# Widths of the node ranges of edge tiles: fixed for blocks of 32 edge tiles instead of 128

## The chip, the cores and the metric

The kernel runs on one core of a Trainium2 chip. A core has a matmul engine (TensorE: PE in the profile, with its weight loads as PEld), a vector engine (VectorE: DVE), a scalar engine (ScalarE: ACT), a general engine (GpSimd: POOL) and a queue engine that issues transfers (SyncE: SP). Data lies in HBM (DRAM), in SBUF (128 partitions) and in PSUM, where matmuls write[...]. The metric is the device time of one execution in microseconds (us); of several runs the median counts.

## The reference, cut to what matters

A graph with 6250 nodes of 256 features and 100,000 edges goes through three relational layers (8 edge types) and one attention layer, each with a residual sum and a layer norm. All values are fp32. The edges are sorted by `dst`, and `dst` is 6250 times the square of a uniform number: low nodes have many edges, high nodes few.

```python
dst = jnp.minimum((6250 * jax.random.uniform(...) ** 2.0).astype(jnp.int32), 99999)
_o = jnp.argsort(dst, stable=True)
src = src[_o]; dst = dst[_o]
...
for l in range(n_layers):                       # 3 layers
    xr = jnp.einsum('nd,rde->rne', x, W_rel[l])
    msg = xr[edge_type, src]
    agg = jax.ops.segment_sum(msg, dst, num_segments=x.shape[0])
    x = jax.nn.relu(agg + x @ W_root[l] + bias[l])
```

After the layers: `x = layernorm(x0 + x)`, then attention with 4 heads over the first 6250 edges, `x = layernorm(x + attention)`.

## The kernel before

**Tiles and windows.** The 100,000 edges are cut into T = 782 edge tiles of 128 edges. Because edges are sorted by `dst`, the 128 edges of one tile end in a short range of nodes. The kernel gives each tile a window: W neighbouring node numbers, from the tile's least `dst` on. For a tile the kernel gathers the 128 source rows (128 x 256, one indirect DMA from POOL), builds a one-hot matrix of 128 edges x (8 types x W nodes), and multiplies: rows transposed times one-hot. That sums the rows by type and node. The product, 2 halves of 128 features x 8 W columns, is then added into a ring `S` in SBUF at the place of the tile's first node. When all edge tiles of a node tile (128 nodes) have been added, a dense step multiplies the sums with the weights of the 8 types and with the root weight.

**Widths.** W must be known when the program is built. `Plan.W` holds one width per chunk of 128 edge tiles (CH = 7 chunks). It takes the density of nodes at the chunk's last edge, times 128 edges, plus five standard deviations and 2 (lines 56 to 60). For this graph the list is 6, 10, 14, 18, 21, 25, 26. `WMAX` is 26. Four places read it: the one-hot (line 474), the window matmuls (499), the add (517), and the tables: `wm` (W - 1 for each tile, lines 303 to 305), which bounds the window's start (`most`, line 312) and enters the test for tiles whose edges don't fit (line 400), and the key of an edge, type x W + node within the window (line 356). If any tile doesn't fit, a flag sends the program into a second, general path after the fast one. The first 36 tiles (TH) are not done in windows but through a count matrix `A` (`count`, `products`), so windows are made for 746 tiles.

**Order.** `Plan.order` puts the tiles into groups of four (GT), 188 groups, high tiles first, and alternates two streams: f = 0 has tiles 410 to 781, f = 1 has tiles 36 to 409; each stream has its own ring (4 and 3 node tiles long). The order is the same in each of the three layers and the layers are issued one after another in the written order (`manual_schedule`). Before the layers, `tables` computes indices, keys and positions; its instructions are ordered by the framework.

In step i of a layer (loop at line 774) the kernel issues:
- four gathers on POOL (`gather`, line 492) into one of eight `msg` buffers, and the positions of the four windows (`places`);
- on DVE the one-hot of the group four steps later (`onehot`, line 476);
- what follows finished dense steps (`finish`: bias, relu, store; in the last layer a layer norm too), and clearing the ring's rows on ACT;
- on PE the window matmuls of group i (`windows`, line 509), into banks `pw`, of which there are four. As many windows share a bank as fit, rounded down to 4, 2 or 1 (lines 501 and 502): 4 for W up to 8, 2 for W up to 16, else 1;
- a piece of the waiting dense steps (`dense`, lines 573 and 577, into `pd`);
- on DVE the four adds into the ring (`add`, line 521);
- transposes and the start of new dense steps for node tiles that have become complete.

The last layer has more on PE and DVE (`logits`, and from step 164 on `prepare`, which takes `msg` buffers and `pw` banks too). `products` loads node rows into `msg` buffers from step 130 on. The gathers of a layer read the table that the layer before has stored. After the layers comes `attention`.

Of the kernel before, what the change touches and what calls it, by code (L numbers as in the profile page):

```python
# [10 lines left out]
F32 = mybir.dt.float32  # L11
# [3 lines left out]
ALU = mybir.AluOpType  # L15
# [5 lines left out]
P = 128  # L21
# [11 lines left out]
DB = 32  # L33
PREP_AT = 164
PIECE = 6
AHEAD = 4
LEAD = 6
GWIN = 256
# [4 lines left out]
class Plan:  # L43
# [7 lines left out]
    def __init__(self, N, E, R):  # L51
        self.N, self.E = N, E
        self.NT = (N + P - 1) // P
        self.T = (E + P - 1) // P
        self.CH = (self.T + P - 1) // P
        self.W = []
        for c in range(self.CH):
            f = min(1.0, (c + 1) * P * P / E)
            step = 2.0 * N * f / E
            self.W.append(min(PAD, math.ceil(P * step + 5 * math.sqrt(P) * step + 2)))  # L60
        self.WMAX = max(self.W)

        self.TH = 0
        while self.hot_high(self.TH) < HOT - 0.01:
            self.TH += 1
        self.TH -= self.TH % GT


        mid = (self.T + self.TH) // 2
        self.TM = min(range(mid - 16, mid + 16),  # L70
                      key=lambda t: (len(self.shared(t)), abs(t - mid)))
# [86 lines left out]
def fast(tc, const, pl, x, xs, src, dst, edge_type, w_rel, w_root, bias, weight,  # L158
# [10 lines left out]
    with ExitStack() as top:  # L169
# [26 lines left out]
        with tc.tile_pool(name="ps_p", bufs=2, space=PSUM) as ps_p:  # L196
            tables(tc, pl, ps_p, src, dst, edge_type, ident, idx, key, pos, iota, iota_p,
                   lane, hk, hl, hif, dt, flag, R, H)
        y = dram.tile([NT * P, D], F32, name="y")

        with ExitStack() as s:
            wp = s.enter_context(tc.tile_pool(name="wp", bufs=1))
            sp = s.enter_context(tc.tile_pool(name="sp", bufs=1))
            mp = s.enter_context(tc.tile_pool(name="mp", bufs=8))
            op = s.enter_context(tc.tile_pool(name="op", bufs=AHEAD + 2))
            xp = s.enter_context(tc.tile_pool(name="xp", bufs=3))
# [44 lines left out]
def tables(tc, pl, ps_t, src, dst, edge_type, ident, idx, key, pos, iota, iota_p, lane, hk, hl,  # L251
           hif, dt, flag, R, H):

    nc = tc.nc
    E, NT, T, CH, WMAX = pl.E, pl.NT, pl.T, pl.CH, pl.WMAX
    TF = E // P
    with tc.tile_pool(name="prep", bufs=1) as prep:
# [29 lines left out]
        sf, df, tf = flt  # L287
# [5 lines left out]
        def turned(o, f, c0, c1):  # L293
            pt = ps_t.tile([P, 4 * P], F32, name="pt")
            for c in range(c0, c1):
                nc.tensor.transpose(pt[:, (c - c0) * P:(c - c0 + 1) * P], f[:, c], ident)
            nc.vector.tensor_copy(o[:, c0 * P:c1 * P], pt[:, :(c1 - c0) * P])
# [3 lines left out]
            turned(idx, sf, c0, c1)  # L301

        wm = prep.tile([P, CH], F32, name="wm")
        for c in range(CH):
            nc.vector.memset(wm[:, c:c + 1], float(pl.W[c] - 1))

        lim = float(pl.N) / float(E) ** 2
        most = prep.tile([P, CH], F32, name="most")
# [23 lines left out]
        def place(o, c0, c1):  # L332

            m0, m1 = pl.TM // P, (pl.TM + P - 1) // P
            if min(c1, m1) > c0:
                remainder(o[:, c0:min(c1, m1)], c0, min(c1, m1), NS[1])
            if c1 > max(c0, m1):
                remainder(o[:, max(c0, m1):c1], max(c0, m1), c1, NS[0])
            if m0 < m1 and c0 <= m0 < c1:
                up = prep.tile([P, 1], F32, name="up")  # L340
                m = prep.tile([P, 1], F32, name="m")
                remainder(up, m0, m1, NS[0])
                nc.vector.tensor_scalar(m, tn[:, m0:m1], float(pl.TM) - 0.5, None, op0=ALU.is_gt)
                nc.vector.tensor_tensor(up, up, o[:, m0:m1], ALU.subtract)
                nc.vector.scalar_tensor_tensor(o[:, m0:m1], up, m, o[:, m0:m1],
                                               op0=ALU.mult, op1=ALU.add)

        for c0, c1 in parts:
            nc.vector.tensor_copy(df[:, c0:c1], raw[1][:, c0:c1])
            nc.scalar.copy(tf[:, c0:c1], raw[2][:, c0:c1])  # L350
            nc.vector.tensor_reduce(lo[:, c0:c1], df[:, c0:c1], AX.X, ALU.min)
            nc.vector.tensor_tensor(
                sf[:, c0:c1], df[:, c0:c1],
                lo[:, c0:c1].unsqueeze(2).to_broadcast([P, c1 - c0, P]), ALU.subtract)
            for c in range(c0, c1):
                nc.vector.scalar_tensor_tensor(sf[:, c], tf[:, c], float(pl.W[c]), sf[:, c],
                                               op0=ALU.mult, op1=ALU.add)
            turned(key, sf, c0, c1)

            nc.vector.tensor_tensor(at[:, c0:c1], lo[:, c0:c1], least[:, c0:c1], ALU.max)  # L360
            nc.vector.tensor_tensor(at[:, c0:c1], at[:, c0:c1], most[:, c0:c1], ALU.min)
            place(posf, c0, c1)
            pr = ps_t.tile([P, 4 * P], F32, name="pt")
            for c in range(c0, c1):
                nc.tensor.matmul(pr[0:1, (c - c0) * P:(c - c0 + 1) * P], posf[:, c:c + 1], ident,
                                 start=True, stop=True)
            nc.vector.tensor_copy(pos[0:1, c0 * P:c1 * P], pr[0:1, :(c1 - c0) * P])
# [28 lines left out]
        b = prep.tile([P, CH], F32, name="b")  # L396
# [59 lines left out]
def layer(tc, pl, l, final, groups, ready, S, hold, A, hk, hl, idx, key, pos, iota, ident, wr, wo,  # L456
          bias_b, x, xs, eps, w1x, altab, y, att, mp, op, xp, hp, ps_w, ps_d, ps_t, H):
    nc = tc.nc
    N, D = x.shape
    KC = D // P  # L460
    R = wr.shape[2]
# [9 lines left out]

    def onehot(i):
        g = groups[i][1]
        w = R * pl.W[g[0] // P]
        oh = op.tile([P, GT, R * pl.WMAX], F32, name="oh")
        nc.vector.tensor_tensor(  # L476
            oh[:, :len(g), :w], iota[:, :w].unsqueeze(1).to_broadcast([P, len(g), w]),
            key[:, g[0]:g[-1] + 1].unsqueeze(2).to_broadcast([P, len(g), w]), ALU.is_equal)
        return oh

    def places(i):
        f, g = groups[i]
        _, v = nc.values_load_multi_w_load_instructions(
            pos[0:1, g[0]:g[-1] + 1], engines=[DVE], min_val=0, max_val=NS[f] * P - 1,
            skip_runtime_bounds_check_because="a remainder of the ring's size")
        return v
# [9 lines left out]

    def windows(i, msg, oh):
        g = groups[i][1]
        w = R * pl.W[g[0] // P]

        nb = 512 // (KC * w)
        nb = 4 if nb >= 4 else 2 if nb >= 2 else 1
        res = []
        for n, (q, t) in enumerate(reversed(list(enumerate(g)))):
            if n % nb == 0:
                pb = ps_w.tile([P, 512], F32, name="pw")
            pw = pb[:, (n % nb) * KC * w:(n % nb + 1) * KC * w]
            for k in range(KC):
                nc.tensor.matmul(pw[:, k * w:(k + 1) * w], msg[:, q, k * P:(k + 1) * P],  # L509
                                 oh[:, q, :w], start=True, stop=True)  # L510
            res.append((q, t, pw))
        return res

    def add(i, wins, vals):
        f, g = groups[i]
        n = NS[f]
        W = pl.W[g[0] // P]
        for q, t, pw in wins:
            a, b = pl.touched(t)
            o = S[f][:, :, ds(vals[q], W)]  # L520
            ins = nc.vector.tensor_tensor(  # L521
                o, o, pw.rearrange("p (a b) -> p a b", b=W), ALU.add)
            for j in done[f][-n:]:
                assert j > b
                if all((j - m) % n for m in range(a, b + 1)):
                    tc.declare_no_dep(ins.ins, group=f"used{l}_{f}_{j}",
                                      reason="the window lies in other node tiles of the ring")
            for h, j in ready:
                assert (h != f or j <= b or j in done[f]
                        or j % n not in [m % n for m in range(a, b + 1)])  # L530
# [233 lines left out]
    for j, (i, f) in last.items():  # L764
        early.setdefault(max(0, i - 2), []).append(j)
    held, turned, xTs = {}, [], {}
    ohs = [onehot(i) for i in range(min(AHEAD, NG))]
    fin, log = [], []
    counting = count() if l == 0 else iter(())
    hot = products()  # L770
    prep = prepare() if final else iter(())
    if final:
        nc.vector.memset(altab, 0.0)
    for i in range(NG + 5):
# [10 lines left out]
        if i < NG:  # L785
            msg = gather(i)
            vals = places(i)
        if i + AHEAD < NG:
            ohs.append(onehot(i + AHEAD))
        for j, yt in [t for k, t in log if k <= i - 2]:  # L790
# [8 lines left out]
        if i < NG:  # L799
            wins = windows(i, msg, ohs.pop(0))  # L800

        n = PIECE * max(1, len(turned)) if i < NG else KC * (R + 1)
        while turned and n > 0:
# [4 lines left out]
        if i < NG:  # L808
            add(i, wins, vals)
# [519 lines left out]
```

## Time and profile before

| what | value |
|---|---|
| median of 3 runs | 3013.36 us (3005.31 to 3019.54) |
| the profiled execution | 3008.72 us, its span 3007.0 us |
| mean granted TensorE clock | 0.941 |
| ACT busy | 462.7 us (15%) |
| mean DMA rate | 129 GB/s |

The stages can be read from the first and last gather of each layer and from the share of time in which the engines are busy. Layer 0 gathers from 11.0 to 947.4 us, layer 1 from 968.3 to 1902.8, layer 2 from 1923.5 to 2883.5; attention and the end take the rest to 3007. The page's forty slices show the same: PE stays at nine tenths or more for most slices, with dips at the two layer boundaries and in the end.

```profile
PE   5999999999987799999988988789999999998874
POOL 6777777777775777777777777577767777777723
PEclk9999999999988999999999987899999999999875
```

Each digit is the busy share of a slice of 75 us in tenths. "Idle before" in the groups and the view of waits name what ended an engine's idle time; "issue" there means that the engine waited for nothing that the profile shows. The chain of waits is followed back from the last instruction; its shares name the engine that each stretch of it was spent on.

### The profile page before, as it was taken

Reading aid. Unit: us, or ns where it says so; the run is one execution under the profiler, and the core shown is the slowest. Engines: PE = TensorE matmul, PEld = TensorE weight load, DVE = VectorE, ACT = ScalarE, POOL = GpSimd, SP = SyncE. Lnnn points to the kernel's source line nnn. Section 1 sums busy time; section 2 is a strip of 40 time slices with the busy share of each in tenths; the row PEclk is TensorE's granted clock in tenths of the full one; section 3 lists DMA queues with packets and bytes.
Section 4 is the critical chain, followed back from the end, with each engine's and each line's share of the span. In section 5 each row is a group of like instructions: output and inputs, shape, how many; then the busy total and the mean of one; then the engine's idle time right before and its main releaser. Section 6 shows DMA issues by size and latency. Waiting matters only on the chain.

```text
span 3007.0 us, 45570 instructions
## 1 busy us (share of the span) xinstructions
PE 2692.7 (90%) x15710; PEld 2444.4 (81%) x15711; DVE 1735.3 (58%) x4084; ACT 462.7 (15%) x611; POOL 2158.3 (72%) x2258
## 2 busy tenths in 40 slices
PE   5999999999987799999988988789999999998874
PEld 4989888889876798999877887688888888888763
DVE  7646677775443555555455444356666656655775
ACT  2111111111001111111111110011111111111015
POOL 6777777777775777777777777577767777777723
PEclk9999999999988999999999987899999999999875
DMA  4444444445433444444444543344444444455523
GB/s 151 125 124 122 120 117 122 120 134 172 134 114 116 119 123 120 125 122 122 119 118 146 166 125 114 118 124 127 131 120 128 123 127 127 152 169 153 167 89 130
DMA packets 203055, 389.00 MB, mean 129 GB/s; under 512 B 42885, under 2 KB 128004, under 8 KB 202820
## 3 DMA queue, kind: packets, MB, share of 16 engines
q0 software_dynamic: 107424, 293.48, 33.6%
q1 hardware_dynamic: 87464, 85.04, 8.8%
q10 hardware_dynamic: 7932, 7.48, 0.7%
q8 instruction: 131, 2.15, 0.3%
q14 instruction: 104, 0.85, 0.1%
HBM read 360.18 MB, written 25.65 MB: 128 GB/s over the span
## 4 chain that ended last, share of the span: by engine, by line
PE 74%; POOL 6%; issue 6%; DVE 6%; DMA 5%; ACT 2%; DVEq 0%; ACTq 0%; POOLq 0%; SPq 0%
PE pw L509 34%; PE pd L577 31%; POOL msg L492 6%; PE pd L573 4%; DMA msg<-x,idx 3%; DVE S L521 3%; PE pd L681 1%; PE pt L544 1%; DMA msg<-in_x_dram,idx 1%; PE pt L625 1%; ACT xT L547 1%; ACT o L1028 1%; PE pd L652 1%; DVE oh L476 0%; PE p L1006 0%
## 5 line engine op out<-in xcount | busy, mean ns | idle before, releaser
L492 POOL DMA_INDIRECT msg<-x,idx x1492 | 1417.9, 950 | 518.2 <-issue 409.4
L521 DVE TENSOR_TENSOR S<-S,pw 128x224 f32 (+6 forms) x2238 | 953.8, 426 | 947.4 <-PE pd L577 519.4
L509 PE MATMUL pw<-oh,msg 128*128 128x112 f32 (+6 forms) x8952 | 1337.4, 305 | 176.8 <-DMA msg<-x,idx 89.1
L509 PEld LDWEIGHTS pw<-oh,msg 128*128 128x128 f32 x8952 | 1272.6, 200 | 247.6 <-DVE S L521 108.8
L577 PE MATMUL pd<-wr,S 128*128 128x256 f32 x4704 | 1103.7, 385 | 1.3 <-DVE S L521 1.3
L577 PEld LDWEIGHTS pd<-wr,S 128*128 128x128 f32 x4704 | 892.2, 193 | 117.3 <-DVE S L521 2.5
L492 POOL DMA_INDIRECT msg<-in_x_dram,idx x746 | 708.6, 950 | 237.8 <-issue 204.4
L476 DVE TENSOR_TENSOR oh<-iota,key 128x672 f32<-128x672 f32 (+8 forms) x564 | 388.2, 690 | 20.6 <-issue 9.8
L586 ACT ACTIVATE S<-S 128x2048 uint32<-128x2048 uint32 x150 | 285.0, 1900 | 0.1
L547 ACT COPY xT<-pt 128x256 f32<-128x256 f32 x195 | 72.3, 371 | 1001.3 <-PE pt L544 1001.3
L594 ACT ACTIVATE h<-pd 128x256 f32<-128x256 f32 x98 | 37.6, 384 | 915.2 <-DVE pd L591 735.1
L573 PE MATMUL pd<-wo,xT 128*128 128x256 f32 x588 | 164.9, 405 | 3.8 <-ACT h L594 3.8
L591 DVE TENSOR_TENSOR pd<-pd,bias_b 128x256 f32<-128x256 f32 x147 | 63.0, 428 | 168.9 <-PE pd L577 168.7
L573 PEld LDWEIGHTS pd<-wo,xT 128*128 128x128 f32 x588 | 108.5, 201 | 13.2 <-ACT h L594 4.3
L643 DVE TENSOR_SCALAR sel<-iota,hk 128x392 bf16<-128x392 f32 x138 | 80.3, 613 | 0.0
L608 ACT ACTIVATE rs<-mv,eps 128x1 f32<-128x1 f32 x49 | 14.4, 295 | 418.9 <-DVE mv L607 418.9
L681 PE MATMUL pd<-msg,A 128*128 128x256 f32 x294 | 70.3, 381 | 1.7 <-DMA msg<-x 1.7
L1010 POOL TENSOR_TENSOR z<-yg,td 128x1536 f32<-128x1536 f32 (+1 forms) x9 | 29.4, 3274 | 56.7 <-DVE bn L988 28.0
L681 PEld LDWEIGHTS pd<-msg,A 128*128 128x128 f32 x294 | 54.6, 192 | 8.5 <-issue 2.0
L544 PE MATMUL pt<-ident,xin 128*128 128x128 f32 x294 | 58.2, 281 | 1.9 <-ACT xT L547 1.4
L625 PEld LDWEIGHTS pt<-w1x,xT 128*128 128x128 f32 x192 | 25.4, 193 | 35.1 <-ACT xT L547 35.1
L544 PEld LDWEIGHTS pt<-ident,xin 128*128 128x128 f32 x294 | 41.7, 146 | 13.6 <-ACT xT L547 2.6
(186 smaller groups left out, 671.7 us busy)
## 6 DMA issues: line engine op xcount, KB each, us to landing
msg<-x,idx POOLq DMA_INDIRECT x1492
x<-h SPq DMA_DIRECT2D x96, 128.0 KB
xin<-x SPq DMA_DIRECT2D x96, 128.0 KB
msg<-x SPq DMA_DIRECT2D x24, 512.0 KB
msg<-in_x_dram,idx POOLq DMA_INDIRECT x746
y<-yt SPq DMA_DIRECT2D x49, 128.0 KB
wr<-in_L_gnn_W_rel_dram ACTq DMA_DIRECT2D x6, 1024.0 KB
xin<-in_x_dram SPq DMA_DIRECT2D x48, 128.0 KB
```

The lines of the kernel that those rows point to most:

```text
L476: nc.vector.tensor_tensor(oh[:, :len(g), :w], iota[:, :w].unsqueeze(1).to_broadcast([P, len(g), w]), key[:, g[0]:g[-1] + 1].unsqueeze(2).t ...
L492: nc.gpsimd.indirect_dma_start(out=msg[:, q, :], out_offset=None, in_=table, in_offset=bass.IndirectOffsetOnAxis(ap=idx[:, t:t + 1], axis=0))
L509: nc.tensor.matmul(pw[:, k * w:(k + 1) * w], msg[:, q, k * P:(k + 1) * P], oh[:, q, :w], start=True, stop=True)
L521: ins = nc.vector.tensor_tensor(o, o, pw.rearrange("p (a b) -> p a b", b=W), ALU.add)
L544: nc.tensor.transpose(pt[:, k * P:(k + 1) * P], t[:, k * P:(k + 1) * P], ident)
L547: nc.scalar.copy(xT.rearrange("p k n -> p (k n)"), pt[:, :D])
L573: nc.tensor.matmul(pd[:, :D], xT[:, k], wo[:, k], start=(k == 0), stop=False)
L577: i = nc.tensor.matmul(pd[:, :D], s[:, k * R + r], wr[:, k, r], start=False, stop=(k == KC - 1 and r == R - 1))
L586: i = nc.scalar.memzero(cols(f, j))
L591: nc.vector.tensor_tensor(pd[:, :D], pd[:, :D], bias_b[:, l], ALU.add)
L643: nc.vector.tensor_scalar(oh, iota[:, :NT * R], float(512 * n), hk[:, t:t + 1], op0=ALU.add, op1=ALU.is_equal)
L681: nc.tensor.matmul(ph[:, :D], A[:, j], t[:, n], start=(n == 0), stop=(j == js[-1]))
```

## The change

The widths are fixed for blocks of 32 edge tiles (WB = 32) instead of chunks of 128. `Plan.W` now has 28 entries, by the same formula, with the density at the block's last edge: 3, 4, 5, ... rising by about one a block to 26. All readers index it with the tile divided by 32. Since one column of the tables holds 128 tiles on the partitions, `wm` is filled with one memset of 32 partitions for each block, 28 in place of 7, and a new column table `wn` (W itself) takes the place of the number in the key's formula. WMAX, the order of the groups, the streams and the positions of everything else stay. Groups of four tiles never cross a block.

The widths of the tiles that are done in windows, block by block, and how many windows share a bank:

| tiles | W before | W after (blocks of 32) | windows in a bank, before -> after |
|---|---|---|---|
| 36-127 | 6 | 4, 5, 6 | 4 -> 4 |
| 128-255 | 10 | 7, 8, 9, 10 | 2 -> 4, 4, 2, 2 |
| 256-383 | 14 | 11, 12, 13, 14 | 2 -> 2 |
| 384-511 | 18 | 15, 16, 17, 18 | 1 -> 2, 2, 1, 1 |
| 512-639 | 21 | 19, 20, 20, 21 | 1 -> 1 |
| 640-767 | 25 | 22, 23, 24, 25 | 1 -> 1 |
| 768-781 | 26 | 26 | 1 -> 1 |

```diff
+WB = 32
...
-        for c in range(self.CH):
-            f = min(1.0, (c + 1) * P * P / E)
+        for c in range(self.CH * P // WB):
+            f = min(1.0, (c + 1) * WB * P / E)
             step = 2.0 * N * f / E
             self.W.append(min(PAD, math.ceil(P * step + 5 * math.sqrt(P) * step + 2)))
...
         wm = prep.tile([P, CH], F32, name="wm")
-        for c in range(CH):
-            nc.vector.memset(wm[:, c:c + 1], float(pl.W[c] - 1))
+        for b, w in enumerate(pl.W):
+            p0 = b * WB % P
+            nc.vector.memset(wm[p0:p0 + WB, b * WB // P:b * WB // P + 1], float(w - 1))
+        wn = prep.tile([P, CH], F32, name="wn")
+        nc.vector.tensor_scalar(wn, wm, 1.0, None, op0=ALU.add)
...
-                nc.vector.scalar_tensor_tensor(sf[:, c], tf[:, c], float(pl.W[c]), sf[:, c],
+                nc.vector.scalar_tensor_tensor(sf[:, c], tf[:, c], wn[:, c:c + 1], sf[:, c],
                                                op0=ALU.mult, op1=ALU.add)
...
     def onehot(i):
         g = groups[i][1]
-        w = R * pl.W[g[0] // P]
+        w = R * pl.W[g[0] // WB]
...
     def windows(i, msg, oh):
         g = groups[i][1]
-        w = R * pl.W[g[0] // P]
+        w = R * pl.W[g[0] // WB]
...
     def add(i, wins, vals):
-        W = pl.W[g[0] // P]
+        W = pl.W[g[0] // WB]
```

## The prediction

> **What bounds the kernel now.** I read the page first, then the waits of POOL layer by layer, then short stretches of the timeline where POOL stood still, and last the groups by shape, for prices.
>
> ```profile
> PE 2692.7 (90%) x15710; PEld 2444.4 (81%) x15711; DVE 1735.3 (58%) x4084; ACT 462.7 (15%) x611; POOL 2158.3 (72%) x2258
> PE 74%; POOL 6%; issue 6%; DVE 6%; DMA 5%; ACT 2%; DVEq 0%; ACTq 0%; POOLq 0%; SPq 0%
> L492 POOL DMA_INDIRECT msg<-x,idx x1492 | 1417.9, 950 | 518.2 <-issue 409.4
> ```
>
> Busy shares and the chain of waits both say TensorE. But the last line has the gathers of layers 1 and 2 (L492), and behind its 0.95 us each stands idle time that is put down to "issue": POOL waited for nothing. The timeline shows a fixed rhythm, 0.95 us busy and 0.30 us of issue, so a gather costs 1.25 us. There are 746 edge tiles in each of three layers, 2238 gathers: 2238 x 1.25 = 2798 us of the 3007 us span, 93%. The waits of POOL, first in layer 1 (969 to 1903 us), then in layer 2 (1924 to 2884 us), with columns total us, times, longest:
>
> ```profile
> POOL msg L492 <- issue: 208.6, 684, 0.6
> POOL msg L492 <- DMA wr<-in_L_gnn_W_rel_dram: 20.0, 1, 20.0
> POOL msg L492 <- PE pw L509: 10.1, 33, 0.3
> ...
> POOL msg L492 <- issue: 200.7, 659, 0.3
> POOL msg L492 <- PE pw L509: 30.1, 43, 4.2
> POOL msg L492 <- DMA wr<-in_L_gnn_W_rel_dram: 19.7, 1, 19.7
> POOL msg L492 <- DMA msg<-x,idx: 7.8, 14, 3.9
> POOL msg L492 <- PE pt L544: 6.0, 11, 2.4
> ```
>
> In layer 1 no wait but the layer boundary is longer than 0.6 us: waits on PE of at most 0.3 us are the issue gap itself under another name. So POOL never stood still for PE there: 745 intervals took 934.5 us (968.32 to 1902.85), 1.254 each. Layer 0 took 936.4 (11.03 to 947.40). Layer 2 took 960.0 (1923.54 to 2883.53), 25 more, and there POOL does wait for PE, up to 4.2 us:
>
> ```profile
> 2238.39 0.94 POOL L492 DMA_INDIRECT msg<-x,idx  x1 [3.96 <-PE pw L509]
> ```
>
> The gathers write eight `msg` buffers; a ninth group has to wait until the windows matmuls have read the oldest. So PE sets the pace only where it is eight groups behind. From the starts of all gathers I add up what each interval has above 1.25 us: layer 0, 1.8 us (387 to 470 us); layer 1, nothing; layer 2, 10.0 us between 2219 and 2369, 3.3 at 2592 and 2653, and 10.9 from 2806 on, after `prepare` has begun to take `msg` buffers too. That is 26 us in all, the most that a faster PE or DVE can take out of the gather stream. The rest (11.0 us head, two boundaries of 20.9 and 20.7, 123.5 from the last gather to the end) is no matter of window widths, but for some tenths.
>
> **What the Trainium skill says.** Perfetto Trace Analysis, Identifying the Most-Contended Engine, takes occupancy as the measure for GPSIMD and warns against matmul busy time. The warning fits; the occupancy (72%) does not: with the issue gaps POOL is at 93%. TensorE: Matmul & The Clock Gate, Back-to-back issue gap, says that in a stream of load and matmul pairs both set the spacing; so there should be a floor below which fewer columns save nothing. The trace agrees; start, duration, and groups of 16 records (four tiles, two matmuls each, two records a matmul):
>
> ```profile
> 309.03 2.87 PE L509 MATMUL pw<-oh,msg 128*128 128x200 f32 x16
> 395.58 2.44 PE L509 MATMUL pw<-oh,msg 128*128 128x168 f32 x16
> 1714.31 2.12 PE L509 MATMUL pw<-oh,msg 128*128 128x144 f32 x16
> 302.06 1.93 PE L509 MATMUL pw<-oh,msg 128*128 128x112 f32 x16
> 1709.93 1.88 PE L509 MATMUL pw<-oh,msg 128*128 128x48 f32 x16
> ```
>
> From 144 to 200 columns it is (2.87 - 2.12)/56 = 0.0134 us a column and group; below some 130 columns ((2.12 - 1.93)/0.0134 = 14 less than 144) it is flat. VectorE: DVE Perf Modes, The TRN2 errata, gives an fp32 tensor_tensor as (N + 151)/0.96 ns: 574 and 257 for 400 and 96 elements. The trace has 571 and 257, so this prices widths that the trace lacks; the same form at 800 elements took 985 against 991:
>
> ```profile
> L521 DVE TENSOR_TENSOR S<-S,pw 128x400 f32 x384 | 219.2, 571 | 248.6 <-PE pd L577 214.7 <-PE pw L509 10.9 <-DVE S L521 0.5
> L476 DVE TENSOR_TENSOR oh<-iota,key 128x800 f32<-128x800 f32 x96 | 94.5, 985 | 3.2 <-issue 0.2
> L521 DVE TENSOR_TENSOR S<-S,pw 128x96 f32 x276 | 70.9, 257 | 127.4 <-PE pw L509 119.7 <-DVE S L521 0.5
> ```
>
> PSUM — Partial Sum Buffer, PSUM bank collisions, asks that PE and VectorE be kept apart by bank, not by address. That makes the number of windows in one `pw` bank matter: at W = 6 (four in a bank) the add starts at 1711.85, when the last of the 16 matmuls has ended (1709.93 + 1.88).
>
> **The change part by part.** Matmuls: with 8 groups in a block of 32 tiles, columns fall above the floor only in these blocks (old to new columns, us a layer): tiles 384-415 and 416-447, 144 to 120 and 128, counted to 130, 1.5 each; 448-479, 144 to 136, 0.9; 512-543, 168 to 152, 1.7; 544-575 and 576-607, 168 to 160, 0.9 each; 640-671, 200 to 176, 2.6; 672-703, 200 to 184, 1.7; 704-735, 200 to 192, 0.9. Sum 12.6 us a layer, 38 for three. Tiles below 384 are at the floor already: their narrower windows give PE nothing.
>
> Adds and one-hots: mean W falls from 16.33 to 15.01 over 746 tiles, 984 units a layer. An add loses 16 elements a unit, a one-hot 8: 984 x 24 / 0.96 ns = 24.6 us a layer, 74 for three, off DVE's 1735. DVE is 58% busy and its idle before the adds is mostly waiting for PE's `pd`, so little of it is on any path: between 2100 and 2370 us PE waited 3.2 us for adds, of which shorter ones give back under 0.5.
>
> What reaches the gathers: layer 0, PE has saved over 4 us before its stalls of 1.8 begin, so all 1.8 go. Layer 1: nothing to take. Layer 2: at the first stall (group 58 of 188) PE has saved blocks 704 and 672, three groups of 640 and the f = 1 groups of 384-415, 4.7 us, by the end of that stretch 6.6; with the adds I take 7 of its 10.0. By group 130 PE has saved 9.8, 3 more, and against 3.3 of stalls I take 2. The last 10.9 lie where PE works at the floor and `prepare` shares the buffers; between 0 and 10.9, and I take 1, because nothing in that stretch gets shorter on PE. Layer boundaries: the last windows of layer 1 start at 1907.12, 4.3 us after the last gather, where a layer's first windows need 3.6 (1924.79 to 1928.38); up to 0.7 us of PE lag each, and I take 0.6 for both. Sum: 1.8 + 7 + 2 + 1 + 0.6 = 12.4 us.
>
> Head: 28 memsets of `wm` instead of 7, one `wn`, and L356 reads a column in place of a number (same pass over 128 elements). Seven memsets took 0.11 us together and DVE then waited for its first input:
>
> ```profile
> 1.27 0.11 DVE L305 MEMSET wm<- 128x1 f32 x7
> 3.52 0.29 DVE L300 CAST flt<-raw 128x256 f32<-128x256 int32 x1 [1.94 <-DMA raw<-in_src_dram]
> 11.03 1.10 POOL L492 DMA_INDIRECT msg<-in_x_dram,idx  x1 [9.11 <-DVE least L318]
> ```
>
> Twenty-one more at the same price are 0.33 us, at 0.06 (the single one of `eps`) 1.3; both fit into the 1.94. `wn` is 0.16, beside the 0.16 of its neighbours. Without that cover all of it would move the first gather and hence everything: 1.5 us. But `tables` is not issued in a written order, and the first gather waits for an `idx` cast that the order puts at 10.33 though its transposes ended at 4.6; another order could bring it up to 5 us sooner or later. I take 0.
>
> Banks: four windows to a bank instead of two in tiles 128-191, two instead of one in 384-447. The adds of such a group start later by 0.95 us (half of 1.9) or some 0.5, but a group then holds one bank of the four instead of two, or two instead of four, so PE waits less for free banks. In the PE-bound stretch these were under 3.2 us. I take 0 and keep both ends for the rival below. Order of groups, gathers, dense matmuls and all queues past POOL, SP and ACT stay: TM and the reaches do not use W.
>
> The profiled execution took 3008.7 (span 3007.0 and 1.7 around it): 3008.7 - 12.4 = 2996.3. It lies 4.6 below the median of the runs, 3013.4; carried over, 3013.4 - 12.4 = 3001.
>
> **The rivals.** First, all 26 us of stalls go, with the boundaries 27: 2986. For it: the stalls are small against 38 us of PE work. Against: two fifths of them lie where PE saves nothing. Second, the chain is right, PE's 38 us come out in full and more with DVE's: 2970 or less. Against it stands layer 1: a stream at 1.25 us a gather with no stall cannot be shortened by PE. Third, stalls stay because buffers and latency cause them: 3011. Fourth, slower: fuller banks delay the adds. Sixteen groups a layer by 0.95 and sixteen by 0.5 are 23 us a layer, 70 in all; it decides once a dense matmul waits for those adds and the lag fills the eight buffers. Half of it, less what is saved, gives 3013 + 35 - 12 = 3036. Against it: PE's waits of `pd` on adds are 1.3 us in the whole span, and between 1200 and 1900 us PE itself waits 43 us for gathers, slack that would have to be used up first. A fifth: a tile too wide for its new range would set the flag and run the general path, many times slower; the widths keep five standard deviations and the given edges stay one node or more inside every new width, so under 1%.
>
> **How the numbers follow.** Forecast (3001, itself 2994 to 3010): 0.58. First rival: 0.22. Second: 0.04. Third: 0.07. Slower, with a bad head order: 0.09. A difference under 0.5%, 15 us, can't be told from no change here. Faster by more: first and second rival and a slice of the forecast's lower side, 0.31; within: 0.60; slower: 0.09. Range 2982 to 3018: it takes in the first rival, the head's 5 us and the spread of the runs.
>
> **What would show it.** Right: layer 1 again some 934.5 us from first to last gather, gathers every 1.25 us, layer 2 shrunk from 960 to about 950, 10 us off the 2219-2369 stalls down to about 3, matmul groups of 2.56 us at 176 columns, DVE busy near 1660. Wrong: a layer 1 shorter than 934 (gathers sped up), waits of PE on adds grown, or a first gather far from 11 us.

## The result and the profile after

The changed kernel took 2999.25 us (median of 13 runs, 2994.72 to 3003.58), the kernel before 3012.77 us (13 runs) beside it. The ratio is 0.9954, with a 95% interval of 0.9944 to 0.9963: 0.46% faster, 13.5 us. The profiled execution has a span of 2993.0 us, 14.0 less than before. The engines' busy times from the page, and the group of the gathers (its line is 496 now):

```profile
PE 2667.7 (89%) x15710; PEld 2424.1 (81%) x15711; DVE 1667.6 (56%) x4106; ACT 462.6 (15%) x611; POOL 2159.9 (72%) x2258
L496 POOL DMA_INDIRECT msg<-x,idx x1492 | 1419.2, 951 | 504.6 <-issue 411.9
```

DVE lost 68 us of work and PE 25 us by its modelled ends, and the span lost 14. A gather still takes 0.95 us. From first to last gather (starts in the timeline), layer 0 took 935.0 us (936.4 before), layer 1 934.4 (934.5), layer 2 946.6 (960.0). So 13.4 of the 14.0 us came out of layer 2. What POOL waited for there (1921 to 2872 us; total, times, longest):

```profile
POOL msg L496 <- issue: 204.5, 671, 0.3
POOL msg L496 <- DMA wr<-in_L_gnn_W_rel_dram: 20.6, 1, 20.6
POOL msg L496 <- PE pw L513: 13.4, 35, 1.4
POOL msg L496 <- DMA msg<-x,idx: 6.8, 16, 2.3
POOL msg L496 <- PE pt L548: 6.2, 10, 3.2
```

The third line was 30.1 us with a longest wait of 4.2. Most of its 35 waits are the issue gap of 0.3; the largest stall between groups 58 and 90 is now this one (before: 3.96, at 2238.39):

```profile
2245.44 0.94 POOL L496 DMA_INDIRECT msg<-x,idx  x1 [1.40 <-PE pw L513]
```

In all that follows "stalls" are what the idle time before each gather of a layer has above 0.30 us, summed over groups 0 to 109, 110 to 159 and 160 to 187, worked out from the starts and durations of all 2238 gathers. Layer 2 before: 10.1, 3.3 and 10.9 us. After: 2.3, 3.5 and 3.6.

The groups of window matmuls have the predicted length. At 176 columns they took 2.55 us (the slope of 0.0134 us a column from 144 up gives 2.55; the prediction had 2.56), and at 192 columns 2.76 us (the slope gives 2.76):

```profile
2055.31 2.76 PE L513 MATMUL pw<-oh,msg 128*128 128x192 f32 x16
...
2251.97 2.55 PE L513 MATMUL pw<-oh,msg 128*128 128x176 f32 x16
```

The head shows the memsets (now L307), the first cast after them, the second one with its wait, and the first gather:

```profile
1.26 2.65 DVE L307 MEMSET wm<- 32x1 f32 x28
4.11 0.29 DVE L301 CAST flt<-raw 128x256 f32<-128x256 int32 x1
5.90 0.56 DVE L301 CAST flt<-raw 128x512 f32<-128x512 int32 x2 [0.85 <-DMA raw<-in_src_dram]
10.97 1.10 POOL L496 DMA_INDIRECT msg<-in_x_dram,idx  x1 [9.04 <-DVE least L322]
```

The 28 memsets took 2.65 us and pushed the first cast from 3.52 to 4.11. The next wait for input, once 1.52 us and now 0.85, took that up, and the first gather started at 10.97 us, as before (11.03).

### The profile page after: what moved, and what is told of

Same layout as the page of the kernel before. It is cut to its first block, busy times and chain, and to the rows that moved or that the text cites. A ratio compares the mean times of both kernels' runs of the same rounds, so it can differ in the third digit from the quotient of the medians.

```text
span 2993.0 us, 45318 instructions
## 1 busy us (share of the span) xinstructions
PE 2667.7 (89%) x15710; PEld 2424.1 (81%) x15711; DVE 1667.6 (56%) x4106; ACT 462.6 (15%) x611; POOL 2159.9 (72%) x2258
## 5 line engine op out<-in xcount | busy, mean ns | idle before, releaser
L513 PE MATMUL pw<-oh,msg 128*128 128x160 f32 (+22 forms) x8952 | 1308.0, 303 | 195.6 <-DMA msg<-x,idx 101.4
L513 PEld LDWEIGHTS pw<-oh,msg 128*128 128x128 f32 x8952 | 1253.8, 202 | 261.2 <-issue 119.9
L525 DVE TENSOR_TENSOR S<-S,pw 128x320 f32 (+22 forms) x2238 | 904.5, 404 | 989.4 <-PE pd L581 508.1
L480 DVE TENSOR_TENSOR oh<-iota,key 128x640 f32<-128x640 f32 (+23 forms) x564 | 363.8, 647 | 26.4 <-issue 14.8
```

The source lines that it names most:

```text
L480: nc.vector.tensor_tensor(oh[:, :len(g), :w], iota[:, :w].unsqueeze(1).to_broadcast([P, len(g), w]), key[:, g[0]:g[-1] + 1].unsqueeze(2).t ...
L525: ins = nc.vector.tensor_tensor(o, o, pw.rearrange("p (a b) -> p a b", b=W), ALU.add)
```

## The experiments

Each run is set against the kernel before, measured beside it on the same chip. The last columns are from one profile each: layer 2 from first to last gather, its stalls by groups as above, and how long prepare's matmuls waited for adds of windows.

| run | ratio to before (95%) | layer 2, us | stalls, us | prepare on adds, us |
|---|---|---|---|---|
| before (profile of the start) | 1 | 960.0 | 10.1, 3.3, 10.9 | 7.3 |
| before again | 1.0007 (0.9998 to 1.0015) | 964.9 | 12.2, 4.6, 13.2 | 7.9 |
| changed | 0.9954 (0.9944 to 0.9963) | 946.6 | 2.3, 3.5, 3.6 | 0 |
| changed again | 0.9957 (0.9942 to 0.9972) | 953.1 | 4.8, 2.6, 7.7 | 0 |
| one window a bank from 384 | 0.998 (0.9967 to 0.9992) | 953.8 | 4.8, 2.9, 7.9 | 7.7 |
| high tiles only | 0.995 (0.9936 to 0.9963) | 946.7 | 4.4, 1.2, 6.1 | 1.1 |
| low tiles only | 0.9994 (0.9984 to 1.0003) | 967.7 | 10.7, 7.7, 13.3 | 7.8 |
| tiles 384-447 only | 0.9978 (0.997 to 0.9986) | 955.0 | 11.6, 4.5, 3.6 | 1.1 |
| windows capped at 16 | 0.9914 (0.9899 to 0.9929) | 940.4 | 0, 0, 3.9 | 0.4 |
| seven msg buffers | 1.0036 (1.0024 to 1.0047) | 970.8 | 10.3, 4.8, 20.4 | 0.4 |
| nine, one-hots 3 ahead | 0.9964 (0.995 to 0.9977) | 949.1 | 0, 3.2, 9.5 | 0 |
| nine, one-hots 4 ahead | 1.0147 (1.0129 to 1.0164) | 950.9 | 0, 1.9, 11.6 | 0 |

**How much one profile says.** First the two kernels once more.

> The kernel before once more, to see how far the stalls of POOL differ from one execution to the next. Theory: they come from the order and the durations of PE and DVE, so they lie at the same groups: some 10 us before group 110 of layer 2, 1.8 in layer 0, none in layer 1; the late ones 9 to 14. Rival: they are chance of the transfers; then they lie elsewhere and differ by more than half.

The early stalls came at the same groups and in the same size, 12.2 us; the late ones were 13.2. Layer 0's 1.8 us did not come back (0), so they were chance.

> The changed kernel once more, on the same chip as the run beside it. Theory: ratio to before 0.994 to 0.997, stalls of layer 2 2 to 5 us before group 110 and 3 to 7 after 160, no wait of prepare's matmuls on adds above 1 us. Rival: the 3.6 us of late stalls in its first profile were luck; then 9 or more.

Early 4.8, late 7.7, no wait of prepare's matmuls on window adds: within the expectation or 0.7 above it. One profile tells the early stalls of the two kernels apart; the late ones only roughly, by 3.6 and 7.7 against 10.9 and 13.2. Where a late stall matters below, the timed ratio decides.

**Does PE set the time at all?** Windows wider than 16 are cut, so their sums leave out some edges.

```diff
+        self.W = [min(16, w) for w in self.W]
...
-        nc.vector.tensor_tensor(bad, a, wm, ALU.is_gt)
+        nc.vector.tensor_scalar(bad, a, float(P), None, op0=ALU.is_gt)
```

> Widths as changed, but none above 16, so every matmul is at the floor; edges beyond a window's 16 nodes are left out of the sums and the test of widths is left out. PE loses another 44 us a layer. Theory: gathers at 1.25 us set the time, so layers 0 and 1 stay at 934 to 935 us from first to last gather and layer 2 goes to 935 to 940; time 2985 to 2993. Rival (PE sets the time, as the chain of waits has it): 130 us less, about 2870.

The ratio puts it at 0.9914 x 3012.77 = 2987 us. Some 130 us of PE work were gone by the slope (79 us of PE's busy time on the page, whose ends are modelled), and DVE had 115 us less to do, yet the kernel was only 12 us faster than the changed one. Layers 0 and 1 took 935.4 and 936.2 us, layer 2 940.4, at most 1.2 us above the expectation. Where the saved time went stands in the waits of PE for gathered rows, first the changed kernel's, then this one's:

```profile
PE pw L513 <- DMA msg<-x,idx: 101.4, 42, 10.9
```

```profile
PE pw L514 <- DMA msg<-x,idx: 168.6, 78, 10.8
PE pw L514 <- DMA msg<-in_x_dram,idx: 59.6, 37, 4.8
```

PE became free and waited: 78 stops in layers 1 and 2 in place of 42, and 60 us in layer 0 in place of 24. The chain of waits, which had 74% of the span on PE, would have put this version near 2870.

**Which tiles bring the gain?** Widths of the tiles below 384 as before, then the other way round.

```diff
+        self.W[:12] = [6] * 4 + [10] * 4 + [14] * 4
```

> Only tiles from 384 up get the new widths; 36-383 keep 6, 10, 14. Theory: below 384 the matmuls are at their floor, so nothing is lost: 2999 within 3, layer 2 946 to 949 us. Rival: shorter adds and one-hots of the low tiles matter in the last stretch, where DVE is busiest: 3003 to 3006.

0.995, the changed kernel's ratio within the intervals: the low tiles add nothing that can be told, though DVE was busy 34 us longer (1701.4 against 1667.6). Their matmuls are at the floor and their adds lie in cover.

```diff
+        self.W[12:] = [18] * 4 + [21] * 4 + [25] * 4 + [26] * 4
```

> Only tiles 36-383 get the new widths; from 384 up 18, 21, 25, 26 as before. Theory: PE saves nothing, the 10 us of stalls between groups 58 and 90 of layer 2 stay, and so do most of the late ones: 3008 to 3013, layer 2 955 to 960 us. Rival (a chain of PE and DVE in which every narrower window counts): half of the gain, 3005 to 3006.

No difference from the kernel before can be told: 0.9994, with 1 in the interval. Layer 2 was longer than expected, and the stalls are back. The timeline has the same one, in size and place, as before the change (2238.39, 3.96):

```profile
2238.42 0.95 POOL L497 DMA_INDIRECT msg<-x,idx  x1 [3.97 <-PE pw L514]
```

**Columns or banks?** A bank is here one `pw` tile of the kernel, 512 fp32 values on each partition. In tiles 384-447 two things change at once: matmuls (and with them adds and one-hots) shrink from 144 columns to the floor, and two windows share a bank in place of one. These tiles are done between groups 1 and 13 and again between groups 163 and 181 of a layer. One run takes the sharing back and keeps all widths.

```diff
         nb = 4 if nb >= 4 else 2 if nb >= 2 else 1
+        nb = 1 if g[0] >= 384 else nb
```

> The changed kernel, but tiles from 384 up keep one window to a bank, as before (384-447 otherwise have two). Theory: in the last stretch of layer 2 the narrow windows helped because a group of four then held two of the four banks and left two for the matmuls of prepare. Taken back, the stalls of POOL after group 160 return (some 11 us instead of 4) and the time is 3004 to 3007, layer 2 from first to last gather 952 to 955 us. Rival: shorter matmuls and adds did it; then 2999 and 947.

0.998, that is 3007 us on the scale above: by the times, the packing is worth (0.998 - 0.9954) x 3012.77 = 8 us (the two intervals leave 3 to 13), the narrower columns the other 6. The profile does not show these 8 us. It is of one of this kernel's faster executions, 3002.47 us where the median is 3010.07, and its late stalls, 7.9, are below the 11 expected and equal to those of the changed kernel's second profile. From the first gather of group 160 to the last one of layer 2 it took 147.3 us. The three profiles with wide windows there took 150.5 to 152.1, and the four with narrow windows, two to a bank, 142.4 to 147.4 (the two of the changed kernel, high tiles only, and tiles 384-447 only). One profile is little to go by, but narrower windows without the packing seem to gain something there too. What the profile does show is the wait on banks. In the kernel before, the matmuls of `prepare` (L738) come after a high group that fills all four banks, and wait until an add frees one. Timelines of PE, before and then with one window a bank:

```profile
2789.22 2.12 PE L509 MATMUL pw<-oh,msg 128*128 128x144 f32 x16
2794.31 2.12 PE L738 MATMUL pw<-al,A 128*128 128x196 bf16 x12 [2.96 <-DVE S L521]
2796.22 3.54 PE L509 MATMUL pw<-oh,msg 128*128 128x48 f32 x16
```

```profile
2792.04 1.95 PE L514 MATMUL pw<-oh,msg 128*128 128x128 f32 x16
2796.94 1.22 PE L743 MATMUL pw<-al,A 128*128 128x196 bf16 x12 [2.96 <-DVE S L526]
2798.00 3.64 PE L514 MATMUL pw<-oh,msg 128*128 128x40 f32 x16
```

The same wait to the hundredth, with narrow windows and shorter adds. And the changed kernel at that place:

```profile
2783.52 1.95 PE L513 MATMUL pw<-oh,msg 128*128 128x128 f32 x16
2785.30 1.18 PE L742 MATMUL pw<-al,A 128*128 128x196 bf16 x12
2789.08 2.71 PE L513 MATMUL pw<-oh,msg 128*128 128x40 f32 x16 [2.60 <-issue]
```

prepare's matmuls find two banks free and run at once. The wait is not gone: the windows behind them now stand still for 2.60 us. The profile gives no releaser; the adds of the high group ran on DVE from 2788.11 on, and the second of them, with which one bank has been read, ended at 2788.98, so that bank is the likely one. But `prepare` now runs beside the wait in place of after it. From the start of one group of windows to the start of the next it is 7.00 us before, 5.96 with one window a bank, 5.56 after; to the end of the next, when its `msg` buffer can be free, 10.54, 9.60 and 8.27 us. At the next place of this kind (2831.14 us before) the last three are 7.87, 7.62 and 7.07. So the packing gave 1.3 and 0.6 us at these two places. The rest of the 8 us was not found in a profile.

The same part alone, put into the kernel before:

```diff
+        v = self.W[12:14]
+        self.W = [6] * 4 + [10] * 4 + [14] * 4 + v + [18] * 2 + [21] * 4 + [25] * 4 + [26] * 4
```

> The kernel before with one part alone: only tiles 384-447 get their new widths, 15 and 16, and with them two windows to a bank. Theory: the matmuls of prepare no longer wait for a bank (7 us of PE waits gone), the late stalls fall from 11-13 to 4-6 us, the early ones by 3 at most: 3 to 8 us faster than before, layer 2 951 to 956. Rival: the late gain needs PE to come less late out of the early stretch; then the late stalls stay near 11 and the time within 3 us of before.

0.9978: 7 us faster (4 to 9 by the interval) with 2 of the 28 widths changed. The early stalls stayed (11.6) and the late ones fell to 3.6. What prepare's matmuls waited for adds, in the kernel before, with one window a bank, and here (total, times, longest):

```profile
PE pw L738 <- DVE S L521: 7.3, 5, 3.0
PE pw L743 <- DVE S L526: 7.7, 5, 3.0
PE pw L744 <- DVE S L527: 1.1, 2, 0.8
```

The rival falls: the late gain does not need a PE that comes less late out of the early stretch. This run shows which tiles bring it. It does not part banks from columns, since both were changed in them.

**Are the buffers the link between PE and POOL?**

```diff
-            mp = s.enter_context(tc.tile_pool(name="mp", bufs=8))
+            mp = s.enter_context(tc.tile_pool(name="mp", bufs=7))
```

> The changed kernel with seven msg buffers instead of eight. Theory: POOL stalls when PE is a buffer count behind, so one group of 5 us less brings stalls where PE's lag was 35 to 40 us: layer 2 before group 110 from 2.3 to 6-8 us, layer 0 from 0 to 1-4, late ones from 4-6 to 8-15, 3008 to 3022. Rival: stalls come from PE's order alone; unchanged within 3 us.

1.0036, 25 us slower than the changed kernel and just beyond the 3022 us expected. The early stalls went from 2.3 to 10.3 us, more than the 6 to 8 expected, the late ones to 20.4, beyond the 15. Layer 0 stalled for 0.4 us, less than expected, layer 1 for none. In the late stretch POOL now waits for DVE's reads of the buffers that `prepare` took, which the changed kernel's waits have hardly at all:

```profile
POOL msg L496 <- PE pw L513: 26.5, 41, 3.6
POOL msg L496 <- DVE A L727: 14.6, 5, 5.6
```

Nine buffers need room; first from the one-hots (AHEAD = 3, bufs = 9).

> The changed kernel with nine msg buffers; to make room for one, one-hots are made three groups ahead instead of four. Theory: the stalls before group 110 of layer 2 (2.3 to 5 us) go, those after 160 fall to about 2, layer 2 936 to 942 us, time 2990 to 2996, faster than both kernels. Rival: later one-hots hold PE up (waits of PE on one-hots grow past 30 us) and the time is 3000 or more.

The early stalls are gone, as expected: 0. The late ones were 9.5 in place of 2 (the changed kernel's two profiles have 3.6 and 7.7), and the ratio, 0.9964, that is 3002 us in place of 2990 to 2996, is no better than the changed kernel's. One-hots are not what PE waits for (3.5 us in all). So the lead was given back and the room taken elsewhere (SELS = 3 in place of 6, one `yt` buffer in place of two).

> The changed kernel with nine msg buffers, one-hots four groups ahead as ever; room comes from three in place of six buffers in the count of layer 0 and one in place of two for the rows that layer 2 stores. Theory: the early stalls of layer 2 stay gone, as with nine buffers before, and the late ones, 9.5 us there, fall back to 3 to 6, because they came of the shorter lead of the one-hots: layer 2 940 to 945 us, 3 to 6 us faster than the changed kernel run beside it. Rival: nine buffers themselves upset the late stretch; then 8 us or more stay there and the time equals the changed kernel's.

Ratio 1.0147, 44 us slower than the kernel before, through a cost that I had not seen. With three `sel` tiles PE waits for DVE in the count of layer 0, and this reaches the gathers: layer 0 took 976.5 us. PE's wait, and one of POOL's:

```profile
PE pd L656 <- DVE sel L647: 56.1, 30, 3.0
...
695.18 0.95 POOL L496 DMA_INDIRECT msg<-in_x_dram,idx  x1 [7.24 <-PE pw L513]
```

Layer 2 can still be read: early stalls 0, late 11.6 with the full lead. So the shorter lead alone is not the cause. The ninth buffer goes with longer late stalls in two kernels of different leads, each with one profile. Why is open (the single `yt` buffer was changed with it). No version tried that sums all edges beat the changed kernel by more than the intervals; high tiles only is its equal.

## Why the prediction was right

The forecast was 3001 us, 12.4 faster, within 2982 to 3018; measured 2999.25, 13.5 faster. A difference under 0.5% was held not to be told from no change; these 0.46% can be, since the interval ends at 0.9963. The bound was read rightly: POOL's gathers at 1.25 us set the time, PE counts only where it is a ring of buffers behind. Layer 1 took 934.4 us where "some 934.5" was forecast, and the capped run showed that far less PE work brings little more. By its own terms:

- **Early stalls of layer 2, 7 of 10 us:** 7.8 (10.1 to 2.3), in the second pair of profiles 7.4 (12.2 to 4.8). Right, and the columns above the floor are what does it: with low tiles alone they stay at 10.7, with tiles 384-447 alone at 11.6. Shorter adds are not what does it: from 2100 to 2370 us PE waited for adds for 3.2 us before and for 3.4 us in both profiles after.
- **Floor at about 130 columns, nothing from the tiles below 384:** right. High tiles alone give 0.995.
- **Adds and one-hots mostly in cover:** right. DVE lost 68 us (74 worked out) and 34 of them, the low tiles', changed no time.
- **Stalls around groups 130 to 143, 2 of 3.3 us:** no gain in the first pair (3.3 to 3.5), 2.0 in the second (4.6 to 2.6). Not settled by two profiles.
- **Late stalls, 1 of 10.9 us, "because nothing in that stretch gets shorter on PE":** mis-sized. They fell by 7.3 and by 5.5 us. Two steps failed. The reason given was wrong by the prediction's own list of blocks: the ten high groups from 163 to 181 are tiles 410-447, whose windows go from 144 columns to 120 and 128. In the timelines above a group of them took 2.12 us before and 1.95 after, and its four adds went from 2.12 to 1.86 us. The other step is the one on banks, "I take 0": I had asked what a group holding two banks in place of four saves in the stretch early in the layer where PE is behind, found under 3.2 us, and not asked it for the late stretch, where `prepare` draws on the same four banks. Its waits on L521 (7.3 us) stood in the trace of before. The two blocks alone gave 7 us and brought the late stalls down to 3.6. The times put 8 us, more than half of the whole gain, on the packing, but no profile shows where they lie, so how the late gain divides between banks and columns stays open.
- **Layer 0, 1.8 us, and the boundaries, 0.6:** layer 0 gave 1.3 in the profile, but its stalls were chance (none in either profile of the second pair). The two boundaries cost 1.1 us more after than before in the first pair, 0.6 less in the second; they lie between 20.7 and 22.8 us in all runs. These small terms were below what a profile shows.
- **Head, 0:** right in the sum (11.03 to 10.97), wrong in the price. Twenty-eight memsets took 2.65 us and not 0.44 to 1.7; they overran the cover named by 0.59 us, and a second wait for input behind it, which I had not counted, took up the rest.

So the total came out closer than its terms, and that is luck. A late gain taken 4.5 to 6.3 us too small was offset in part by small terms up to 2.2 us too large. The rest of the offset is that layer 2 got shorter by 13.4 and 11.8 us in the two pairs of profiles though its stalls fell by 14.9 in both. The slower rival, fuller banks that delay adds, did not come: by the times two windows to a bank in tiles 384-447 are worth 8 us, and four to a bank in tiles 128-191 cost nothing that can be told (low tiles only, 0.9994).

## What to carry to other kernels

An engine with 72% busy share can be the bound: look at whether its rhythm has gaps in which it waits for nothing, and multiply the period by the count. Then the value of any faster engine is the sum of the stalls that it causes on the bound, place by place, and not its own saved time. And a smaller tile does not only shorten its operation: ask how many of a shared set of buffers it now leaves free, and for whom, stretch by stretch.

## What the runs showed of the hardware

- Memsets of one column on 32 partitions took 0.095 us each in a row of 28 (2.65 us), while seven of one column on 128 partitions took 0.11 us together. What makes the difference, the start partition or the number of them, was not tried apart.
- Fp32 window matmuls had a floor: groups of 16 records took 1.88 us at 48 columns and 1.95 at 128, 2.12 at 144, then 0.0134 us a column more, 2.87 at 200.
- A gather of 128 rows of 1 KB took 1.25 us of POOL as the median of each of the twelve profiles, with PE busy from 2589 to 2693 us of the span and DVE from 1552 to 1737: 0.946 or 0.947 us busy and 0.305 us of idle time before the next.
